# Residual buffers ahead of the sums' buffers, and pinned, paired divisions in the last projection of a four-layer graph kernel

## The chip, the cores and the metric

The kernel runs on one core of one Trainium2 chip. The metric is the device time of one execution in microseconds (us); the time before is the median of three runs. The core has TensorE (PE, with its weight loads shown apart as PEld), VectorE (DVE), ScalarE (ACT), GpSimd (POOL) and SyncE (SP); SP, POOL and ACT also issue DMAs.

## The reference

Four layers run over a graph of 3327 nodes with 512 features and a dense 0/1 adjacency `adj`. Each layer is added to its input and normalized over the features:

```python
x = _layernorm(x + _L0_gnn_ref(x, adj, W, a))             # attention, 8 heads x 64
x = _layernorm(x + _L1_gnn_ref(x, adj, W_nb, ...))        # mean of the first 64 neighbours
x = _layernorm(x + _L2_gnn_ref(x, adj, W, a))             # attention, 8 heads x 64, elu
x = _layernorm(x + _L3_gnn_ref(x, adj, W, a))             # attention, 4 heads x 128, elu

# attention, per head
h = x @ W
e = leaky_relu(h @ a1 [:, None] + h @ a2 [None, :], 0.2)
att = softmax(where(adj > 0, e, NEG))
out = att @ h                                             # then elu in L2 and L3
```

So behind each attention a kernel has, per row, the weighted sums and the sum of the weights: it divides, applies elu where there is one, adds the residual and normalizes.

## The kernel before, in words

**Tiles.** The 3327 rows make 26 tiles (NT) of 128 rows by 512 features. A layer's work between two attentions goes over these tiles; the attention itself goes over pairs of source and destination rows and fills most of the time (L405 on DVE, L408 on ACT, L428 and L380 on PE).

**Where sums are kept.** An attention stores its weighted sums, not yet divided, in `hd` in HBM. The reciprocals of the weights' sums lie in `rec` on chip. For the last half of the last heads these come late: partial sums go through `dd` and sixteen small DMAs (`place`, L517) into `pes`, and `finish_sums` (L523 to L538) makes `rec` of them. `Layer.late` holds these two steps, and the next stage calls them when it is at tiles 4 and 8.

**Finishing a group** (`finish_steps`, from L165). For n tiles from t0 it gives a list of steps:
- `load`: for each tile a buffer `h` filled from `hd` and a buffer `xr` filled with the residual, both through L126; xr always on POOL's queue, h on the queue that the caller names.
- `divide(s)`: h times rec on DVE (L181), and with elu an exponential into `e` on ACT (L186).
- `add(s)`: with elu two DVE operations, min(e,1)+xr into xr (L194) and max(h,0)+xr into h (L195); without, one addition (L197).
- `norm_rows` (L147 to L161): per tile bn_stats (L152) and bn_aggr (L153) on DVE; one square root on ACT for the group (L154); reciprocal (L155) and product (L158) on DVE; and per tile an ACT operation (L161) that scales and shifts h in place.

Exponential and square root belong to different function tables of ACT, so a table load stands where it changes from one to the other.

**The last projection** (`third`, from L892) finishes layer 2's sums and makes what layer 3's attention reads. It has 13 turns of two tiles (t0 = 0, 2, ...). In a turn it
1. calls L2.late at t0 = 4 and 8;
2. loads the group t0+6 (`load_group`);
3. for each of the two tiles: stores it as x3 (L133); `project1` (L253 to L263): four PE transposes (L261) into `pt`, an ACT copy to `xT` (L262), and on DVE the column sums `xsum` (L263); after the first tile only, all steps that finish the group t0+2; then `project2` (L266 to L283) of the tile before: 16 matmuls (L271) into two banks `pw`, on ACT an exponential `dc` (L272) and two copies `rc`, `qc` (L275), on DVE two products `vt` (L277), and the store of v (L283);
4. at tile 14 prepares the first half of the attention (`prepare` L304 to L322, `cut` L324 to L351, `rows` L359).
After the loop come `mean` (L286 to L293) and the attention of layer 3.

The pool `p_f` holds the groups: ten buffers for h, six for xr, two for e.

**What sets the order.** PE's instructions run in the order of the program: `tc.manual_schedule` names PE alone. On the other engines a planner orders them by estimated times when the kernel is built, and they run in that order. `tc.keep_in_program_order(ins)` pins one instruction: on its engine, what is written before it stays before and what is written after it stays after. In `finish_steps` the flag `pinned` pins the exponential of a group's first tile; `third` sets it for the group of tiles 2 and 3 only. A buffer's address is given when its tile is allocated, in the order of the program; a transfer into it waits for whatever last used these addresses.

**The same helper elsewhere.** The second layer's first step (`step1`, `step2`, from L721) finishes layer 0's sums with `finish_steps`, two tiles at a time, without elu and unpinned; layer 3's own end (`later`, from L957) uses it for the first half of the rows. In the first of these, PE transposes a finished tile (L724) and multiplies it with two matrices (L732, L735).

Of the kernel before, what the change touches and what calls it, by code (L numbers as in the profile page):

```python
# [7 lines left out]
F32 = mybir.dt.float32  # L8
# [5 lines left out]
ALU = mybir.AluOpType  # L14
# [4 lines left out]
P = 128  # L19
# [13 lines left out]
def kernel(  # L33
# [10 lines left out]
    nc = tc.nc  # L44
    N, F = x.shape
# [59 lines left out]
    for e in range(2):  # L105
        nc.vector.tensor_tensor(c1w[:, :, e, :], c1[:, :, 8 * e:8 * e + 4], c1[:, :, 8 * e + 4:8 * e + 8],
                                op=ALU.add)
# [4 lines left out]
    rec = const.tile([P, NT, 8], F32, name="rec")  # L112
# [6 lines left out]
    def load_tile(dst, src, t, eng):  # L119

        if src.shape[0] == N and t == NT - 1 and LAST < P:
            nc.gpsimd.memset(dst, 0.0)
            for a, z in _row_pieces(LAST):
                eng.dma_start(out=dst[a:z, :], in_=src[t * P + a:t * P + z, :])
        else:
            eng.dma_start(out=dst, in_=src[t * P:(t + 1) * P, :])  # L126

    def store_tile(dst, src, t, eng):
        if dst.shape[0] == N and t == NT - 1 and LAST < P:
            for a, z in _row_pieces(LAST):  # L130
                eng.dma_start(out=dst[t * P + a:t * P + z, :], in_=src[a:z, :])
        else:
            eng.dma_start(out=dst[t * P:(t + 1) * P, :], in_=src)  # L133
# [7 lines left out]
    def load_wide(t, src, eng):  # L141
        for e in range(2):
            eng.dma_start(out=t[:, :, e, :FW], in_=src[:, e * FW:(e + 1) * FW].rearrange("(c p) m -> p c m", p=P))


    def norm_rows(pool, ys, t0):
        n = len(ys)  # L147
        st = pool.tile([P, 4, 6], F32, name="st")
        mv = pool.tile([P, 4, 2], F32, name="mv")
        rs = pool.tile([P, 4, 2], F32, name="rs")  # L150
        for s, y in enumerate(ys):
            nc.vector.bn_stats(out=st[:, s, :], in_=y)  # L152
            nc.vector.bn_aggr(out=mv[:, s, :], in_=st[:, s, :])  # L153
        nc.scalar.activation(rs[:, :n, 0], mv[:, :n, 1], AF.Sqrt, bias=eps)  # L154
        nc.vector.reciprocal(rs[:, :n, 0], rs[:, :n, 0])  # L155
        if t0 + n == NT:
            nc.vector.tensor_tensor(rs[:, n - 1, 0:1], rs[:, n - 1, 0:1], valid, op=ALU.mult)
        nc.vector.scalar_tensor_tensor(rs[:, :n, 1], mv[:, :n, 0], -1.0, rs[:, :n, 0],  # L158
                                       op0=ALU.mult, op1=ALU.mult)
        for s, y in enumerate(ys):  # L160
            nc.scalar.activation(y, y, AF.Identity, bias=rs[:, s, 1:2], scale=rs[:, s, 0:1])  # L161
# [3 lines left out]
    def finish_steps(pool, xin, layer, t0, n, hbufs=6, eng=nc.sync, xbufs=None, xpool=None, ebufs=None, pinned=False):  # L165
        H, D = layer.H, layer.D
        ys, xs, steps = [], [], []

        def load():
            for t in range(t0, t0 + n):  # L170
                h = pool.tile([P, F], F32, name="h", bufs=hbufs)
                load_tile(h, hd, t, eng)
                ys.append(h)
                xr = xpool.tile([P, F], F32, name="xr", tag="hb") if xpool else \
                    pool.tile([P, F], F32, name="xr", bufs=xbufs)
                load_tile(xr, xin, t, nc.gpsimd)
                xs.append(xr)

        def divide(s):
            h = ys[s]  # L180
            nc.vector.tensor_tensor(h.rearrange("p (h d) -> p h d", h=H), h.rearrange("p (h d) -> p h d", h=H),  # L181
                                    rec[:, t0 + s, :H].rearrange("p (h e) -> p h e", e=1).to_broadcast([P, H, D]),
                                    op=ALU.mult)
            if layer.elu:
                e = pool.tile([P, F], F32, name="e", bufs=ebufs)
                ins = nc.scalar.activation(e, h, AF.Exp)  # L186
                if pinned and s == 0:
                    tc.keep_in_program_order(ins)
                xs.append(e)

        def add(s):
            h, xr = ys[s], xs[s]
            if layer.elu:
                nc.vector.scalar_tensor_tensor(xr, xs[n + s], 1.0, xr, op0=ALU.min, op1=ALU.add)  # L194
                nc.vector.scalar_tensor_tensor(h, h, 0.0, xr, op0=ALU.max, op1=ALU.add)  # L195
            else:
                nc.vector.tensor_tensor(h, h, xr, op=ALU.add)  # L197

        steps.append(load)
        for s in range(n):  # L200
            steps += [lambda s=s: divide(s), lambda s=s: add(s)]
        steps.append(lambda: norm_rows(pool, ys, t0))
        return ys, steps

    def finish(*a):
        ys, steps = finish_steps(*a)
        for f in steps:
            f()
        return ys
# [682 lines left out]
    def third(first):  # L892
        with tc.tile_pool(name="col3", bufs=1) as cp, tc.tile_pool(name="at_r3", bufs=2, reuse_waits="tile") as rp:
# [3 lines left out]
            with tc.tile_pool(name="p_w", bufs=1, reuse_waits="tile") as wp, \  # L897
                    tc.tile_pool(name="p", bufs=3, reuse_waits="tile") as pp, \
                    tc.tile_pool(name="p_f", bufs=2, reuse_waits="tile") as fp, \
                    tc.tile_pool(name="p_ps", bufs=2, space=PSUM, reuse_waits="tile") as ps:  # L900
                wsb = wp.tile([P, FC, 2, FW + L3.H], F32, name="wsb")

                def bank(e):
                    return ps.tile([P, 512], F32, name=f"pw{e}")


                pend = None
                ahead = first
                groups = []

                def load_group(t0):
                    if t0 < NT:
                        groups.append(finish_steps(fp, x2, L2, t0, 2, 10, nc.gpsimd if t0 < 4 else nc.sync, 6,
                                                    pinned=t0 == 2))
                        groups[-1][1].pop(0)()

                load_group(2)
                load_wide(wsb, w3, nc.gpsimd)
                nc.vector.tensor_copy(wsb[:, :, :, FW:], wa[3].rearrange("p c (e h) -> p c e h", e=2))
                load_group(4)  # L920
                for t0 in range(0, NT, 2):
                    ys = ahead
                    if t0 in (4, 8):
                        L2.late.pop(0)(fp)
                    load_group(t0 + 6)
                    for s, y in enumerate(ys):
                        t = t0 + s
                        store_tile(x3, y, t, nc.sync)
                        xT = L3.project1(pp, ps, y, t)
                        if s == 0 and groups:  # L930
                            ahead, steps = groups.pop(0)
                            for f in steps:
                                f()
                        if pend:
                            L3.project2(pp, bank, wsb, *pend)
                        pend = (xT, t)
                        if t == HALF + 1:
                            L3.prepare(pp, 0)
                            L3.first_rows = L3.rows(rp, 0, 0)
                            L3.cut(pp, 0)  # L940
                L3.project2(pp, bank, wsb, *pend)
                L3.mean(pp, bank, wsb)
# [282 lines left out]
```

## Time and profile before

| | |
|---|---|
| median of 3 runs | 3392.79 us (3391.16 to 3394.97) |
| the profiled execution | 3389.15 us, span 3387.4 us |
| mean granted clock of PE | 0.985 |
| busy, share of the span | PE 96%, PEld 48%, DVE 79%, ACT 70%, POOL 7% |
| L405 on DVE | 1040 times, mean 1954 ns |
| L428 on PE | 8320 matmuls, mean 521 ns |
| L271 on PE, all projections | 1248 matmuls, mean 397 ns |
| L154 table loads | 45, mean 1283 ns |

Times in the timeline count from the start of the span. The last projection starts at about 2551 us (its first transposes, L261, at 2555.88) and its last matmul (L293) ends at about 2688 us: some 4% of the span. The layer that finishes L0's sums starts at about 958 us.

In a line of the timeline the first number is the start, the second the duration, then engine, line, operation, what is written and read, shapes, how many of them follow one another, and in brackets the idle time ahead of it and what ended it. In a line of groups the first figure after the count is busy time, the next the mean of one, and after the bar come idle time and its releasers.

### The profile page before, as it was taken

Reading aid. Unit: us, or ns where it says so; the run is one execution under the profiler, and the core shown is the slowest. Engines: PE = TensorE matmul, PEld = TensorE weight load, DVE = VectorE, ACT = ScalarE, POOL = GpSimd, SP = SyncE. Lnnn points to the kernel's source line nnn. Section 1 sums busy time; section 2 is a strip of 40 time slices with the busy share of each in tenths; the row PEclk is TensorE's granted clock in tenths of the full one; section 3 lists DMA queues with packets and bytes.
Section 4 is the critical chain, followed back from the end, with each engine's and each line's share of the span. In section 5 each row is a group of like instructions: output and inputs, shape, how many; then the busy total and the mean of one; then the engine's idle time right before and its main releaser. Section 6 shows DMA issues by size and latency. Waiting matters only on the chain.

```text
span 3387.4 us, 47182 instructions
## 1 busy us (share of the span) xinstructions
PE 3251.2 (96%) x18476; PEld 1626.4 (48%) x18476; DVE 2687.5 (79%) x2619; ACT 2354.6 (70%) x2143; POOL 239.8 (7%) x389
## 2 busy tenths in 40 slices
PE   8899999999979999999989999999998999999997
PEld 7634344444434445545544444444446754455453
DVE  5799999999967544444449999999998766668887
ACT  2398998999953333333338999999997655558986
POOL 3100000000010011111110000000002000010110
PEclk9999999999999999999999999999998999999998
DMA  9644111110143343333320111111117411122211
GB/s 368 222 124 127 49 49 38 55 49 28 44 123 125 122 117 84 91 85 87 80 77 20 47 48 50 51 48 47 35 31 241 152 41 42 41 51 80 94 42 49
DMA packets 288014, 284.29 MB, mean 84 GB/s; under 512 B 107492, under 2 KB 223534, under 8 KB 287791
## 3 DMA queue, kind: packets, MB, share of 16 engines
q1 hardware_dynamic: 254063, 170.62, 16.6%
q0 software_dynamic: 28208, 102.96, 9.5%
q10 hardware_dynamic: 5520, 7.69, 0.7%
q8 instruction: 146, 2.39, 0.3%
q14 instruction: 77, 0.63, 0.1%
HBM read 212.01 MB, written 69.17 MB: 83 GB/s over the span
## 4 chain that ended last, share of the span: by engine, by line
PE 85%; DVE 5%; DMA 4%; ACT 3%; issue 2%; SPq 0%; ACTq 0%; DVEq 0%; POOL 0%; POOLq 0%
PE po L428 52%; PE acc L859 12%; PE pd L380 7%; PE pw L271 5%; DVE t L405 3%; PE pz L732 3%; DMA raw<-in_adjT_dram 3%; PE pi L735 3%; ACT y L408 1%; PE pt L456 1%; PE pk L819 1%; DMA h<-hd 0%; PE pa L1108 0%; PE pt L724 0%; PE pct L664 0%
## 5 line engine op out<-in xcount | busy, mean ns | idle before, releaser
L405 DVE SCALAR_TENSOR_TENSOR t<-rb,qc,mask 128x1664 f32<-128x1664 f32 x1040 | 1960.3, 1954 | 169.4 <-PE po L428 147.3
L408 ACT ACTIVATE y<-t,bi,sc 128x1664 fp8e4<-128x1664 f32 x1040 | 1769.5, 1766 | 310.4 <-PE pd L380 292.7
L428 PE MATMUL po<-t,vj 128*64 128x448 f32 (+3 forms) x8320 | 1909.6, 521 | 22.1 <-DVE t L405 19.6
L428 PEld LDWEIGHTS po<-t,vj 128*64 128x64 f32 (+1 forms) x8320 | 838.9, 148 | 970.6 <-issue 704.0
L859 PE MATMUL acc<-zs,kt 128*128 128x512 bf16 x1352 | 401.1, 380 | 0.0
L271 PE MATMUL pw<-wsb,xT 128*128 128x264 f32 (+1 forms) x1248 | 302.2, 397 | 15.2 <-DVE vt L277 12.0
L859 PEld LDWEIGHTS <-kt 128*128 128x128 fp8e4 x2002 | 196.1, 98 | 242.1 <-issue 7.7
L811 ACT CAST pk<-cy 128x512 f32<-128x512 bf16 x169 | 99.0, 588 | 277.4 <-DVE kt L823 266.3
L271 PEld LDWEIGHTS pw<-wsb,xT 128*128 128x128 f32 x1248 | 241.1, 197 | 60.7 <-ACT xT L262 10.8
L380 PE MATMUL pd<-y,sden 128*32 128x448 fp8e4 (+1 forms) x4160 | 259.5, 342 | 10.4 <-ACT y L408 10.4
L859 PE MATMUL acc<-zl,kt 128*128 128x512 bf16 x650 | 246.5, 379 | 0.0
L380 PEld LDWEIGHTS <-sden 128*32 128x32 bf16 x4160 | 117.5, 96 | 162.5 <-issue 139.8
L823 DVE SCALAR_TENSOR_TENSOR kt<-pk,mask 128x512 fp8e4<-128x512 f32 x169 | 116.1, 688 | 94.0 <-PE pk L819 94.0
L277 DVE TENSOR_TENSOR vt<-pw,dc 128x256 f32<-128x256 f32 x156 | 59.0, 418 | 148.2 <-ACT dc L272 143.7
L359 POOL DMA_DIRECT2D rb<-r x40 | 21.3, 532 | 1670.4 <-DVE t L405 1652.2
L275 ACT COPY rc<-pw 128x8 f32<-128x8 f32 (+1 forms) x78 | 12.6, 162 | 156.6 <-PE pw L271 154.1
L831 DVE SCALAR_TENSOR_TENSOR y<-acc,cnt,bnb 128x512 f32<-128x512 f32 x26 | 19.5, 751 | 97.7 <-PE acc L859 90.3
L732 PE MATMUL pz<-wn,xT 128*128 128x512 f32 x208 | 94.9, 600 | 1.7 <-ACT xT L726 1.7
L700 POOL DMA_DIRECT2D cy<-ctd x91 | 67.9, 746 | 385.1 <-ACT pk L811 312.6
L735 PE MATMUL pi<-wl,xT 128*128 128x512 f32 x208 | 93.5, 592 | 0.0
L634 DVE TENSOR_SCALAR mask<-raw 128x832 fp8e4<-128x832 int32 (+2 forms) x90 | 54.8, 614 | 38.9 <-DMA raw<-in_adjT_dram 38.5
L154 ACT ACT_TABLE_LOAD x45 | 57.7, 1283 | 37.0 <-DVE mv L153 36.4
(187 smaller groups left out, 1699.3 us busy)
## 6 DMA issues: line engine op xcount, KB each, us to landing
vj<-v SPq DMA_DIRECT2D x312, 128.0 KB
rb<-r POOLq DMA_DIRECT2D x40, 832.0 KB, 4.8
raw<-in_adjT_dram SPq DMA_DIRECT2D x67, 416.0 KB
cy<-ctd POOLq DMA_DIRECT2D x78, 256.0 KB, 4.0
h<-hd SPq DMA_DIRECT2D x61, 256.0 KB
v<-vt SPq DMA_DIRECT2D x50, 256.0 KB
hd<-hb SPq DMA_DIRECT2D x48, 256.0 KB
xr<-x POOLq DMA_DIRECT2D x45, 256.0 KB, 3.1
```

Of the source, the lines that this page charges most:

```text
L271: nc.tensor.matmul(pw[e][:, :FW + H], xT[:, c, :], wsb[:, c, e, :], start=c == 0, stop=c == FC - 1)
L277: nc.vector.tensor_tensor(vt[:, hs, :], pw[e][:, :FW].rearrange("p (h d) -> p h d", d=D), self.dc[:, t, hs].rearrange("p (h e) -> p h e", e=1)
L380: nc.tensor.matmul(pd[c][32 * kk:32 * kk + 32, :w_], lhsT, rhs, start=(kk, c) not in seen, skip_group_check=final is not None, stop=last a ...
L405: nc.vector.scalar_tensor_tensor(t, rb[k], self.qc[:, j, h:h + 1], mask[:, j, i0:i0 + IW], op0=ALU.max, op1=ALU.mult)
L408: nc.scalar.activation(y, t, AF.Sigmoid, bias=self.bi[:, j, h:h + 1], scale=self.sc[:, j, h:h + 1], saturate=False)
L428: nc.tensor.matmul(po[c][k * D:(k + 1) * D, :z - a_], vj[:, j % 2, k * D:(k + 1) * D], ts[k][:, a_:z], start=j == 0, stop=j == NT - 1)
L700: nc.gpsimd.dma_start(out=cy[:, :n, :], in_=ctd[t:t + n, b * GW:(b + 1) * GW] .rearrange("(o t) i -> o t i", o=1).to_broadcast([P, n, GW]))
L732: nc.tensor.matmul(pz, xT[:, c, :], wn[:, c, :], start=c == 0, stop=c == FC - 1)
L735: nc.tensor.matmul(pi, xT[:, c, :], wl[:, c, :], start=c == 0, stop=c == FC - 1)
L811: nc.scalar.copy(pks[k % 2], carry[b, t // 4 * 4][:, t % 4:t % 4 + 2, :])
L823: nc.vector.scalar_tensor_tensor(kt, pk, NEIGHBOURS, mask[:, t:t + 2, i0:i0 + GW], op0=ALU.is_le, op1=ALU.mult, saturate=False)
L859: nc.tensor.matmul(acc, kts[t][:, s * P:(s + 1) * P], zs(t, c) if c < 2 else zl[:, t, :], start=t == 0 and c == 0, stop=t == NT - 1 and c ...
```

## The change

In `load` the residual's buffer `xr` is allocated before `h`; the DMAs are issued in the same order as before. With `pinned`, the steps of a group run as divide, divide, add, add instead of divide, add, divide, add, and the division on DVE is pinned for every group but the first (t0 > 2); the exponential is pinned for tile 2 alone, as before. `third` passes `pinned=True` for all its groups. Lines below `add` stand five further down than before (L194 and L195 two, L186 two).

```diff
@@ -168,23 +168,25 @@
 
         def load():
             for t in range(t0, t0 + n):
+                xr = xpool.tile([P, F], F32, name="xr", tag="hb") if xpool else \
+                    pool.tile([P, F], F32, name="xr", bufs=xbufs)
                 h = pool.tile([P, F], F32, name="h", bufs=hbufs)
                 load_tile(h, hd, t, eng)
                 ys.append(h)
-                xr = xpool.tile([P, F], F32, name="xr", tag="hb") if xpool else \
-                    pool.tile([P, F], F32, name="xr", bufs=xbufs)
                 load_tile(xr, xin, t, nc.gpsimd)
                 xs.append(xr)
 
         def divide(s):
             h = ys[s]
-            nc.vector.tensor_tensor(h.rearrange("p (h d) -> p h d", h=H), h.rearrange("p (h d) -> p h d", h=H),
-                                    rec[:, t0 + s, :H].rearrange("p (h e) -> p h e", e=1).to_broadcast([P, H, D]),
-                                    op=ALU.mult)
+            ins = nc.vector.tensor_tensor(h.rearrange("p (h d) -> p h d", h=H), h.rearrange("p (h d) -> p h d", h=H),
+                                          rec[:, t0 + s, :H].rearrange("p (h e) -> p h e", e=1).to_broadcast([P, H, D]),
+                                          op=ALU.mult)
+            if pinned and t0 > 2:
+                tc.keep_in_program_order(ins)
             if layer.elu:
                 e = pool.tile([P, F], F32, name="e", bufs=ebufs)
                 ins = nc.scalar.activation(e, h, AF.Exp)
-                if pinned and s == 0:
+                if pinned and (t0, s) == (2, 0):
                     tc.keep_in_program_order(ins)
                 xs.append(e)
 
@@ -197,8 +199,11 @@
                 nc.vector.tensor_tensor(h, h, xr, op=ALU.add)
 
         steps.append(load)
-        for s in range(n):
-            steps += [lambda s=s: divide(s), lambda s=s: add(s)]
+        if pinned:
+            steps += [lambda s=s: divide(s) for s in range(n)] + [lambda s=s: add(s) for s in range(n)]
+        else:
+            for s in range(n):
+                steps += [lambda s=s: divide(s), lambda s=s: add(s)]
         steps.append(lambda: norm_rows(pool, ys, t0))
         return ys, steps
 
@@ -911,7 +916,7 @@
                 def load_group(t0):
                     if t0 < NT:
                         groups.append(finish_steps(fp, x2, L2, t0, 2, 10, nc.gpsimd if t0 < 4 else nc.sync, 6,
-                                                    pinned=t0 == 2))
+                                                    pinned=True))
                         groups[-1][1].pop(0)()
 
                 load_group(2)
```

In the built programs the instructions of PE have the same order. On DVE, ACT, POOL and SP the order differs within `third` alone; ACT has two more table loads, the other engines the same number of instructions.

## The prediction

> **What bounds the kernel now.** First the page's header and its chain of work that ended last: TensorE (PE) carries the kernel, and the line the change is about shows only in the 5% and 4% that VectorE (DVE) and DMA hold.
>
> ```profile
> span 3387.4 us, 47182 instructions
> PE 85%; DVE 5%; DMA 4%; ACT 3%; issue 2%; SPq 0%; ACTq 0%; DVEq 0%; POOL 0%; POOLq 0%
> ```
>
> A mean over the span says nothing of the last projection, so next the table of busy time in 20 us windows over it (columns: window, length, PE, PEld, DVE, ACT, POOL busy with instruction counts, granted PE clock, DMA share, GB/s).
>
> ```profile
> 2560.00:2580.00 20.00, 11.54 (x37) 9.09 (x36) 15.96 (x36) 13.13 (x23) 2.88 (x6) 0.64 0.88 274
> 2580.00:2600.00 20.00, 20.00 (x102) 17.25 (x101) 18.50 (x44) 16.51 (x34) 3.22 (x6) 1.00 0.82 270
> 2640.00:2660.00 20.00, 20.00 (x103) 17.41 (x102) 17.86 (x48) 17.15 (x40) 1.06 (x2) 1.00 0.67 228
> 2660.00:2680.00 20.00, 20.00 (x103) 17.37 (x103) 8.85 (x17) 8.68 (x25) 0.00 (x0) 1.00 0.25 96
> ```
>
> Only the first window leaves PE idle. After 2580, PE is full, and in the last window DVE has fallen to 8.85 of 20: it finished the normalization of the last tiles before PE needed them. The steady stage is PE's, because DVE and ScalarE (ACT) run ahead. The timeline of PE shows the stage's rhythm and its one large hole.
>
> ```profile
> 2559.27 5.79 PE L271 MATMUL pw<-wsb,xT 128*128 128x260 f32 x14 [0.30 <-DMA wsb<-in_w_dram]
> 2573.51 1.12 PE L261 MATMUL pt<-ident,h 128*128 128x128 f32 x4 [8.46 <-ACT h L161]
> ...
> 2664.64 0.60 PE L261 MATMUL pt<-ident,h 128*128 128x128 f32 x4
> 2665.08 3.67 PE L271 MATMUL pw<-wsb,xT 128*128 128x260 f32 x16
> 2668.59 0.60 PE L261 MATMUL pt<-ident,h 128*128 128x128 f32 x4
> 2669.03 3.67 PE L271 MATMUL pw<-wsb,xT 128*128 128x260 f32 x16
> 2672.54 0.60 PE L261 MATMUL pt<-ident,h 128*128 128x128 f32 x4
> ```
>
> A tile costs PE 3.95 us (0.44 of transposes, 3.51 of projection), two tiles 7.9. Tile 2 starts 8.46 us late, at 2573.51. Who made it late, says the timeline of DVE:
>
> ```profile
> 2557.77 0.68 DVE L263 TENSOR_REDUCE xsum<-xT 128x4 f32<-128x512 f32 x1
> 2562.96 1.40 DVE L181 TENSOR_TENSOR h<-h,rec 128x512 f32<-128x512 f32 x2 [4.52 <-DMA h<-hd]
> 2564.28 0.69 DVE L194 SCALAR_TENSOR_TENSOR xr<-e,xr 128x512 f32<-128x512 f32 x1
> ```
>
> The two divisions at 2562.96 belong to tiles 4 and 5. The planner put them ahead of tile 2's add at 2564.28, and they wait 4.52 us for a load, though tile 2's own exponential (L186) was done at 2559.62.
>
> **What the Trainium skill says.** "Perfetto Trace Analysis", section "Tensor Engine Instruction (MATMUL, LD_WEIGHTS)", calls ACT, DVE and GpSimd strict FIFOs; the last fence is that, tile 2's ready add behind tile 4's late division. "ScalarE: Activation LUTs", "What ACT_TABLE_LOAD costs": about 1.28 us for a load and about 1.38 of drain at each switch of function set. The trace has the 1283 ns, but no such drain: the load at 2570.74 is followed by its exponential at 2572.04. So I charge 1.28. "TensorE: Matmul & The Clock Gate", "What's actually happening": after an idle window of about 3.4 us PE falls to half clock. Here the 8.46 us hole and the 3.64 us hole at 2634.75 are followed by half-clock work (projections of 5.42 and 5.36 instead of 3.67 us); holes of 0.98 and 1.30 us are not.
>
> **The parts.** Line numbers are those of before.
>
> *Residual's buffer ahead of the sum's.* No instruction is added or moved in time by the program; addresses change, and with them what a load waits for. It bears where the first layer's sums are finished. There the load of tile 2's residual on POOL is issued at 969.73 after 9.92 us of idle time; by the built order it waits for the store of a buffer it lies over. Laid elsewhere it can go at about 960. But DVE's order has a division there that lands at 977.21 after 2.25 us for a load which SP issues only at 972.89, behind six other DMAs, and an add of tile 3 stands behind it. PE's hole of 13.84 us before 983.97 hangs on that. So the earlier residual is hidden; what remains is less traffic beside the late load. I take −1 us; bounds −2 and +1.3 (more traffic before, one landing later).
>
> *The start of the last projection.* Divisions are pinned, so tiles 4 and 5 come after tile 2's and 3's adds. Worked: tile 3's exponential ends at 2560.62; its first add then 2560.65; three more DVE slots of 0.60 for the rest of the adds, two for the statistics, to 2563.65, aggregates to 2563.8. Now ACT's order has the three small copies of tile 0's projection first, and PE ends that at 2565.06: 2565.35 after copies, table load to 2566.65, square root 0.30, reciprocal and product 0.31 with hops to 2567.4, normalization (L161) 0.81: PE starts tile 2 at 2568.3 instead of 2573.51, −5.2 us. Late next is PE's own projection of tile 0, which already fills that time.
>
> *The steady stage.* This is where the pin costs. In program order the division of the next group stands after the column sums (L263) of the current group's first tile. Pinned, it can't pass them, so what let DVE run ahead is gone: PE transposes tile t, the sums of t release the divisions of t+2, and their result is what PE transposes next. One turn per two tiles, with durations from the rows of 2575 to 2635: transposes 0.60, copy (L262) 0.59, sums 0.60, division 0.69, exponential 0.63, four adds and two statistics at a slot of 0.60 = 3.60, aggregate, one L277 at its slot, aggregate 0.17+0.34+0.17, square root 0.30, table load 1.28, dc 0.06, normalization 0.81: 9.84, and six hops of some 0.04 between engines: 10.1 us, against PE's 7.9. The table load for the square root is hidden: ACT has time for it during the adds. A second division or exponential lies beside the first add.
> By ACT's built order this form holds for the groups of tiles 4, 6, 8, 20, 22, 24. For 10, 12, 18 the square root stands behind the three copies of the current tile's projection, so PE must first end both tiles: 7.9+0.16 tail, copies 0.27, table load 1.28, square root 0.30, reciprocal and product 0.31, normalization 0.81, hops: 11.2. For 14, two more exponentials (L316, L307, 0.27 and 0.25) and a table load stand in front: 12.5. For 16, with the rows of L312 between, I keep the 14.84 us of before (2626.13 to 2640.97), since its 3.64 us hole covers the new wait.
> Sum from tile 2 to tile 24: 6×10.1 + 3×11.2 + 12.5 + 14.8 = 121.5, against 2672.54 − 2573.51 = 99.0: +22.5. The tail behind tile 24 and the attention after it keep their lengths. Holes of 2.2 us should not cool PE; those of 3.3 (three) and 4.6 (one) may, at some 1.7 us each (a projection at 5.4 instead of 3.7). I take one, +2; bounds 0 and +7.
>
> *Traffic.* DMAs of the stage are the same in number (x3 stores, h, xr, v) and stretched over a longer stage, with POOL's residual loads waiting on the adds as now (55.5 us of POOL's waits); SP's loads of h are asked for two groups before they are divided. Nothing; at worst a load that is late again, up to the 4.5 us seen.
> *Two at a time, and two more ACT instructions* (table loads): inside the turn above.
>
> **Sum.** −1 −5.2 +22.5 +2 = +18.3 us on a profiled execution of 3389.15 (span 3387.4), giving 3407.5. The median of the three runs shown is 3392.79, 3.6 above it; the same addition gives 3411.1.
> Ends of this case: low if group 16 takes 12.5, no hop costs, no cooling, sums of −2: about +10; high with four cooled projections, no gain in the first layer, 0.2 more per turn: about +27. So 3403 to 3420.
>
> **Rivals.** (1) *Pinning removes the blockage and nothing else* (faster). Mechanism: the turn from transposes to normalization stays under 7.9 us, so PE keeps its rhythm. Then −5.2 −1 = 3386.6, at best 3383 with the 3.64 us hole gone too. For it: DVE has 11 of 20 us free at the end and its total work is unchanged. Against: that freedom came from running ahead; the turn is a latency, with ten dependent steps. It decides at 7.9 us for the turn, 2.2 below my sum.
> (2) *The turn is shorter, only dc binds*: normalization stands on ACT behind dc of the current tile, which needs PE to end it: 7.9 + 0.16 + 0.06 + 0.81 + hops = 9.05 in the six groups. Total 115.2, +16.2, net about +10 to +12: 3404. Same sign; it is the low end.
> (3) *Balance*: some groups still slip past, two or three turns of holes (+6) cancel the start (−5): 3394. Against it: the built order has the same pattern in every group.
> (4) *The first layer gains the whole 9.9 us*: if the late load there followed the residual's. 3402; the order on SP speaks against it. That the change does not do what it says can be left out: the built order shows the moved divisions.
>
> **Chances.** A measurement here can tell about 0.2% (6.8 us) from no change. My case with (2) and (4): 0.79; (3) and other small outcomes 0.09; (1) 0.12. Nearly all of the first is slower by more than 0.2%: slower 0.78, same 0.10, faster 0.12. The likeliest case's own range, 3403 to 3420, holds about 0.70; to leave out no more than 2 in 10 it must reach down over (3) to about 3385, into (1).
>
> **What would show it.** Right: in the changed kernel PE's tile 2 starts about 5 us sooner after tile 1, then a hole of 2 to 4 us before every second group of transposes, put down to ACT h L161, and DVE idle waiting for ACT's xT inside the stage; DVE no longer drops to 8.85 at the end. The last projection's end moves from 2688 by about +18. Wrong: holes under 1 us in the steady stage (then (1)); a PE clock of 0.6 to 0.8 through the whole stage (then above 3420); or a first-layer hole of much less than 13.84.

## The result and the profile after

The changed kernel takes 3413.1 us (median of 4 runs, 3409.88 to 3415.64) against 3392.23 for the kernel before on the same chips (4 runs): ratio 1.0066, 95% interval 1.0054 to 1.0078, so 18 to 26 us slower. The profiled execution has a span of 3408.2 us, 20.8 more than before's 3387.4. Lines from L188 on stand a few further down now: L266 are the transposes, L276 the projection, L268 the column sums, L196 and L197 the adds.

The page's header and chain for the changed kernel:

```profile
span 3408.2 us, 47193 instructions
PE 84%; DMA 5%; DVE 5%; issue 3%; ACT 3%; POOL 0%; SPq 0%; ACTq 0%; POOLq 0%; DVEq 0%
```

Shares over the span hardly move. The windows over the last projection do (same columns as before):

```profile
2580.00:2600.00 20.00, 16.98 (x78) 14.20 (x78) 15.71 (x36) 13.62 (x31) 2.15 (x4) 0.91 0.75 235
2660.00:2680.00 20.00, 15.63 (x71) 13.04 (x72) 14.06 (x32) 14.63 (x28) 0.10 (x1) 0.91 0.38 144
2680.00:2700.00 20.00, 15.89 (x80) 13.29 (x79) 13.36 (x35) 12.65 (x28) 0.00 (x0) 1.00 0.28 105
```

Before, PE was busy for 20.00 of 20 from 2640 to 2680 and DVE fell to 8.85. Now no engine is full: PE has 16 to 17, DVE 13 to 16, ACT 13 to 15. A loop that is bound by latency can look like this: every engine waits for another. The timeline of PE tells where:

```profile
2560.49 5.39 PE L276 MATMUL pw<-wsb,xT 128*128 128x260 f32 x14 [0.56 <-DMA wsb<-in_w_dram]
2569.05 1.12 PE L266 MATMUL pt<-ident,h 128*128 128x128 f32 x4 [3.17 <-ACT h L161]
...
2581.02 0.66 PE L266 MATMUL pt<-ident,h 128*128 128x128 f32 x4 [0.96 <-ACT h L161]
...
2591.18 0.66 PE L266 MATMUL pt<-ident,h 128*128 128x128 f32 x4 [2.05 <-ACT h L161]
2591.68 5.36 PE L276 MATMUL pw<-wsb,xT 128*128 128x260 f32 x16
...
2613.22 1.12 PE L266 MATMUL pt<-ident,h 128*128 128x128 f32 x4 [3.17 <-ACT h L161]
2614.13 6.25 PE L276 MATMUL pw<-wsb,xT 128*128 128x260 f32 x16
...
2640.07 1.12 PE L266 MATMUL pt<-ident,h 128*128 128x128 f32 x4 [4.47 <-ACT h L161]
...
2684.34 0.66 PE L266 MATMUL pt<-ident,h 128*128 128x128 f32 x4 [2.06 <-ACT h L161]
```

The first hole, 8.46 us before, is 3.17: tile 2 starts at 2569.05. Then every second tile, that of group 16 apart, waits for its normalization. In the waits of this stage, first one line of the kernel before, then two of the changed kernel:

```profile
PE pt L261 <- ACT h L161: 11.8, 2, 8.5
```

```profile
PE pt L266 <- ACT h L161: 30.4, 12, 4.5
...
DVE xsum L268 <- ACT xT L267: 10.2, 5, 2.7
```

PE waited 11.8 us in two places before, and 30.4 us in twelve now. The last line is the other half of the loop: DVE stands idle for the transposed tile whose sums release its next divisions. The kernel before shows no such wait of DVE in this stage. Both halves in one turn, DVE first, then ACT:

```profile
2582.42 0.68 DVE L268 TENSOR_REDUCE xsum<-xT 128x4 f32<-128x512 f32 x1
2583.01 1.28 DVE L181 TENSOR_TENSOR h<-h,rec 128x512 f32<-128x512 f32 x2
2584.44 1.29 DVE L196 SCALAR_TENSOR_TENSOR xr<-e,xr 128x512 f32<-128x512 f32 x2
2585.65 1.29 DVE L197 SCALAR_TENSOR_TENSOR h<-h,xr 128x512 f32<-128x512 f32 x2
2586.86 1.28 DVE L152 BATCH_NORM_STATS2 st<-h 128x6 f32<-128x512 f32 x2
```

```profile
2588.65 0.29 ACT L154 ACTIVATE rs<-mv,eps 128x2 f32<-128x2 f32 x1 [1.11 <-DVE mv L153]
2588.96 1.28 ACT L277 ACT_TABLE_LOAD   x1
2590.26 0.17 ACT L277 ACTIVATE dc<-pw 128x4 f32<-128x4 f32 x1
2590.32 1.51 ACT L161 ACTIVATE h<-h,rs 128x512 f32<-128x512 f32 x2
```

From the transposes at 2581.02 through sums, two divisions, four adds, two statistics, square root, table load, dc and normalization to the transposes at 2591.18: 10.16 us.

### The profile page after: what moved, and what is told of

Read it like the earlier page. It is cut to its first block, busy times and chain, and to the rows that moved or that the text cites. A ratio compares the mean times of both kernels' runs of the same rounds, so it can differ in the third digit from the quotient of the medians.

```text
span 3408.2 us, 47193 instructions
## 1 busy us (share of the span) xinstructions
PE 3260.6 (96%) x18476; PEld 1630.8 (48%) x18476; DVE 2687.5 (79%) x2619; ACT 2360.1 (69%) x2145; POOL 239.3 (7%) x389
## 4 chain that ended last, share of the span: by engine, by line
PE 84%; DMA 5%; DVE 5%; issue 3%; ACT 3%; POOL 0%; SPq 0%; ACTq 0%; POOLq 0%; DVEq 0%
PE po L433 52%; PE acc L864 12%; PE pd L385 7%; PE pw L276 5%; DVE t L410 3%; DMA raw<-in_adjT_dram 3%; PE pz L737 2%; PE pi L740 2%; ACT y L413 1%; PE pk L824 1%; PE pt L461 1%; DMA r<-rr 0%; PE pa L1113 0%; PE pt L266 0%; DMA v<-vt 0%
## 5 line engine op out<-in xcount | busy, mean ns | idle before, releaser
L276 PE MATMUL pw<-wsb,xT 128*128 128x264 f32 (+1 forms) x1248 | 308.6, 403 | 13.0 <-DVE vt L282 11.1
L276 PEld LDWEIGHTS pw<-wsb,xT 128*128 128x128 f32 x1248 | 245.7, 200 | 60.7 <-ACT xT L267 9.9
```

The lines of the kernel that those rows point to most:

```text
L276: nc.tensor.matmul(pw[e][:, :FW + H], xT[:, c, :], wsb[:, c, e, :], start=c == 0, stop=c == FC - 1)
```

## The experiments

Each ran on one chip together with runs of the kernel before; differences below are the ratio of the runs, with its 95% interval, times the median of before there (3391.36, 3391.04 or 3389.22 us).

**e1, the layout alone.** In the kernel before, `load` allocates xr ahead of h, as the change does. The built order of every engine is that of before.

> The kernel before with one edit: the residual's buffer is allocated ahead of the sum's. No instruction changes its place in the built order, so only waits of loads change. Main theory: it is worth next to nothing; within 2 us of before (the prediction took -1, with -2 to +1.3 as bounds; the changed kernel's trace, where the hole of PE before the second group of the first layer's finishing is 14.98 us instead of 13.84, points to 0 to +2). Rival, that a part of the 20.9 us comes from the layout: +5 or more. Rival, that the early residual is worth its 9.9 us of waiting and the pins cost 30: -8 or less. In the trace the last projection should be as in before, tile 2 at about 22 us after the stage's first transposes.

Measured: +3.7 us (+1.4 to +6.1), a small cost. The middle value lies between the main theory's 2 us and the rival's 5, and the interval reaches both. The traces put 2.2 us of it in the first layer's finishing (34.92 us from its first transposes to tile 3's instead of 32.70) and 0.2 in the last projection. SP's queue and PE of the kernel before:

```profile
961.81 0.33 SPq L507 DMA_DIRECT2D dd<-red  x1
...
968.92 3.87 SPq L517 DMA_DIRECT2D pes<-dd  x6
```

```profile
983.97 1.11 PE L724 MATMUL pt<-ident,h 128*128 128x128 f32 x4 [13.84 <-ACT h L161]
984.87 4.83 PE L732 MATMUL pz<-wn,xT 128*128 128x512 f32 x8
```

and with the layout alone:

```profile
963.43 0.33 SPq L507 DMA_DIRECT2D dd<-red  x1
...
973.13 3.85 SPq L517 DMA_DIRECT2D pes<-dd  x6
```

```profile
986.85 1.11 PE L724 MATMUL pt<-ident,h 128*128 128x128 f32 x4 [15.09 <-ACT h L161]
987.75 5.79 PE L732 MATMUL pz<-wn,xT 128*128 128x512 f32 x8
```

The loads of tiles 2 and 3 no longer wait on POOL (issued at 960.89 to 962.49). They travel beside the small store dd, and the reading back of dd, for which SP waits, starts 9.70 us after the store instead of 7.11. That the traffic is what delays it is the likely reading, but no run takes the traffic away and keeps the layout. Tile 4's load stands behind that, and DVE's next division behind tile 4's load. PE's hole grows from 13.84 to 15.09, and what follows it runs longer at half clock. The four kernels with the layout and without another edit there have 14.98 to 15.09 (the changed kernel, e1, e4, e6), the three without it 13.84 to 13.94 (before, e2, e5).

**e2, pins and pairs without the layout.** The changed kernel with h allocated ahead of xr again.

> The changed kernel with the layout undone: pins and pairs alone, built order of all engines as in the changed kernel. Main theory: the whole effect is here, +18 to +23 us against before, with the same holes ahead of the transposes of tiles 4, 6, 8, ..., 24 as in the changed kernel (1 to 4.5 us each). Rival, that layout and pins act together: more than 4 us away from the changed kernel's +20.9.

Measured: +21.7 us (+17.6 to +25.8), the holes as in the changed kernel. Pins and pairs together carry the effect; no run has the pairs alone. With e1's +3.7 the sum would be 25.4 where the changed kernel has 22.4; the intervals are too wide to tell whether the two add.

**e4, one group ahead.**

```diff
-                ahead = first
+                done = [first]
...
-                    ys = ahead
+                    ys = done.pop(0)
...
-                        if s == 0 and groups:
-                            ahead, steps = groups.pop(0)
+                        while s == 0 and groups and len(done) < 2:
+                            ready, steps = groups.pop(0)
                             for f in steps:
                                 f()
+                            done.append(ready)
```

> The changed kernel, but a group is finished one turn sooner: in the turn of tiles t0 and t0+1 the steps of group t0+4 run instead of those of t0+2. Pins, pairs and layout stay. Main theory: the cost of the pin is the latency of the turn from transposes to the next normalization (10.1 us against PE's 7.9); spread over two turns it need not be shorter than 15.8, so most of the holes close: 14 to 20 us less than the changed kernel, +1 to +6 against before. What is left are normalizations queued on ACT behind the small copies of the current tile. Rival, that the pinned order costs DVE or ACT throughput (more table loads, colder PE) whatever the distance: within 5 us of the changed kernel.

Measured: +8.8 us (+5.4 to +12.2), 13 to 14 less than the changed kernel. Its timeline of PE:

```profile
2593.89 0.66 PE L266 MATMUL pt<-ident,h 128*128 128x128 f32 x4 [1.48 <-ACT h L161]
2597.89 0.60 PE L266 MATMUL pt<-ident,h 128*128 128x128 f32 x4
2603.47 0.65 PE L266 MATMUL pt<-ident,h 128*128 128x128 f32 x4 [1.48 <-ACT h L161]
```

These two turns are 9.59 and 9.58 us long. The later ones lie between 8.4 and 9.8, the one with the preparation apart (14.90), and from tile 2 to tile 24 it takes 110.1 us (2571.89 to 2681.96) instead of 125.5. The same pins at a distance of two turns cost far less: it is the distance that counts, and throughput falls as a reason. Two misses: the gain is at or just under the low end of what was expected, and the time against before is above it, in part perhaps because the layout's 3.7 us had not been reckoned in. In the first turns the holes that are left end with a normalization that stands on ACT behind the current tile's copies, two table loads and an exponential of a later group. After tile 10's transposes PE waits instead ahead of its projections, mostly for xT and rc on ACT and for vt and mv on DVE.

**e5, hold back only at the start.** The kernel before (its layout, no pins on divisions), with all later divisions of the last projection queued on DVE behind the product L158 of tiles 2 and 3 (`tc.issue_after`). e7 to e11 use the same tie.

```diff
+            with tc.issue_after(gate[0]) if gate and layer.li == 2 else nullcontext():
-            nc.vector.tensor_tensor(h.rearrange(...
+                nc.vector.tensor_tensor(h.rearrange(...
...
+        def norm():
+            last = norm_rows(pool, ys, t0)
+            if pinned:
+                gate.append(last.ins)
```

> The kernel before (no layout, no pairs, no pins on divisions), with all later divisions of the last projection queued on DVE behind the product (L158) of the first group, tiles 2 and 3, and otherwise free. Main theory: the start keeps its gain of about 5 us and DVE may run ahead again after it, so 2 to 5 us less than before, 3387 to 3390; tile 2 starts near 2568.5, and holes afterwards are few. Rival, that the start's gain is taken back by a later wait (the copies of rows in the preparation at tile 14, or a turn that is late): within 1.5 us of before. Rival, that holding back the divisions at the start already costs the later turns: +5 or more.

Measured: +1.4 us (−1.4 to +3.7). The rival holds. Counted from the stage's first transposes, tile 2 comes after 12.53 us (17.63 before), and at tile 14 it is still 3.7 us ahead (66.59 against 70.25). It loses that between tiles 14 and 16:

```profile
2626.22 3.75 PE L280 MATMUL pw<-wsb,xT 128*128 128x260 f32 x16 [1.21 <-DVE vt L286]
2631.74 1.04 PE L321 MATMUL pr<-ident,rc 128*4 128x128 f32 x8 [1.77 <-ACT rc L316]
2636.75 1.23 PE L321 MATMUL pr<-ident,rc 128*4 128x128 f32 x5 [3.98 <-ACT rr L323]
2637.77 1.06 PE L270 MATMUL pt<-ident,h 128*128 128x128 f32 x4
```

It takes 19.07 us from tile 14 to 16 instead of 14.84: the preparation waits for rc and then for rr, which stands on ACT behind another group's square root and normalization. The work after these holes ran in part at half clock.

**e6, no square root.** The changed kernel, with ACT's Identity in place of Sqrt in the last projection's groups: the square root is left out, and with it the change of function table. ACT's order changes too, as the planner orders it anew.

> The changed kernel, in which the square root of the last projection's groups (ACT, L154) is left out: the variance with eps is passed on as it is, so no function table is changed in that stage. Main theory: the turn loses its table loads and keeps the queue on ACT. By the built order the normalization now stands behind the three small copies of the current tile's projection in every group, so a turn is 7.9 of PE + 0.16 tail + copies 0.27 + reciprocal and product 0.31 + normalization 0.81 + hops = about 9.5 us for all groups, instead of 10.1, 11.2 and 12.5, with holes of about 1.6 us: 10 to 17 us less than the changed kernel, and still 4 to 12 above before. Rival, that the latency through DVE is all: the turn falls to some 8.5 us and the time to within 3 us of before. Rival, that table loads are hidden: within 4 us of the changed kernel.

Measured: +5.8 us (+3.1 to +8.5) against before, 14 (by the medians) to 17 (by the ratios) less than the changed kernel.

```profile
2603.27 0.66 PE L266 MATMUL pt<-ident,h 128*128 128x128 f32 x4 [1.54 <-ACT h L161]
2607.27 0.60 PE L266 MATMUL pt<-ident,h 128*128 128x128 f32 x4
2612.92 0.66 PE L266 MATMUL pt<-ident,h 128*128 128x128 f32 x4 [1.54 <-ACT h L161]
```

Seven turns are 9.65 or 9.66 us long where 9.5 was worked out, and after these holes of 1.5 us the projections run at full clock. The number came, but not for the reason given: the copies of the current tile are done at 2602.00, and the normalization waits on for DVE.

```profile
2602.40 1.52 ACT L161 ACTIVATE h<-h,rs 128x512 f32<-128x512 f32 x2 [0.41 <-DVE rs L158]
```

```profile
2601.63 0.67 DVE L268 TENSOR_REDUCE xsum<-xT 128x4 f32<-128x512 f32 x1
2602.22 0.15 DVE L158 SCALAR_TENSOR_TENSOR rs<-mv,rs 128x2 f32<-128x2 f32 x1
```

So the table load is a term of the turn, but the changed kernel's turns of 10.16 and 10.18 us to groups 6 and 22 lose only 0.5 of its 1.28: the load had covered the reciprocal, a column sum and the product on DVE, and without it these end the wait. The turns of 11.3 us lose 1.6 to 1.7, and the half-clock work of the changed kernel's turns that end in groups 8, 12 and 20 is not there.

**e7 to e11, the same fault in the first layer.** The holes of 13.84 to 15 us of e1 hang on a division of tile 4 that stands on DVE ahead of tile 3's addition. e7 is the kernel before with e5's tie in layer 0's finishing instead (divisions of tiles 4 and later behind L158 of tiles 2 and 3); e8 adds the layout; e9 adds e5's tie too. The division and the addition in the kernel before:

```profile
977.21 0.69 DVE L181 TENSOR_TENSOR h<-h,rec 128x512 f32<-128x512 f32 x1 [2.25 <-DMA h<-hd]
977.82 0.68 DVE L197 TENSOR_TENSOR h<-h,xr 128x512 f32<-128x512 f32 x1
```

> The kernel before, its layout too, with one tie in the finishing of layer 0's sums: the divisions of tiles 4 and later stay on DVE behind the product (L158) of tiles 2 and 3. Nothing else. Theory: what makes PE's hole of 13.84 us there is the division of tile 4, which stands on DVE ahead of tile 3's addition and waits for a late load. Without that, tile 3's addition goes when its residual has landed, about 974.8 in the time of the kernel before; statistics, square root, normalization to about 978; tile 2 reaches PE at 978 instead of 983.97: hole about 8, 5 to 7 us less than before. Rival, that the residual's own landing and not the division ends the wait: within 2 us of before.

> As the run before it (tie in the first layer's finishing), with the residual's buffer laid ahead of the sum's. Theory: with the tie, the early residual is no longer hidden. Tile 3's division was at 970.99 in the layout's own run, its addition can follow at once, PE gets tile 2 some 4 us after it ran dry instead of 15: hole 3 to 6 us, 8 to 11 us less than before; a layout that alone cost 4 us then gains 3 to 5. Rival, that the added traffic of the early loads costs whatever the order is: no better than the run without the layout, by 1 to 4 us worse.

> As the run before it, and the same tie in the last projection (divisions of tiles 4 and later behind the product of tiles 2 and 3, no pins after it). Theory: the last projection's tie alone gave nothing (+1.4 us, -1.4 to +3.7: tile 2 started 5.1 us sooner and the preparation's holes took it back), so this is within 3 us of the run before it, 6 to 11 us less than before, faster than both kernels. Rival, that the two gains add: 11 us or more.

Measured: e7 −1.4 us (−4.1 to +1.4), e8 −2.0 (−4.7 to +0.7), e9 −1.7 (−4.4 to +1.0), each less than expected and none clear by itself. The holes did shrink: 13.84 before, 11.09 in e7, 9.16 in e8, 8.80 in e9, so the layout that cost when alone is worth 1.9 us of hole with the tie. Who ends the wait now? In e7 it is in part the rival, the residual's own landing: tile 2's addition waits for it.

```profile
975.64 0.69 DVE L201 TENSOR_TENSOR h<-h,xr 128x512 f32<-128x512 f32 x1 [5.01 <-DMA xr<-in_x_dram]
```

In e8, where the residual is early, it is on ACT:

```profile
974.01 0.30 ACT L770 CAST cf<-cr 26x128 f32<-26x128 bf16 x1 [9.13 <-DMA cr<-ctd]
974.23 0.59 ACT L745 CAST zs<-pz 128x512 bf16<-128x512 f32 x1
```

A small cast, needed only at tile 8, waits for its load, and tile 0's zs behind it; DVE's r and tile 3's addition wait for zs. e10 is e8 with this cast kept in its written place, e11 the same with e5's tie.

```diff
-                        nc.scalar.copy(cf, cr)
+                        tc.keep_in_program_order(nc.scalar.copy(cf, cr))
```

> As the kernel with the first layer's tie and the layout, plus one more tie: the cast of the neighbour counts (cf from cr) on ACT is kept in its written place, at tile 8, where it stood ahead of tile 0's cast zs in the built order and waited 9.13 us for its load, to 974.01, with DVE's r (L747 there) and tile 3's addition queued behind. Theory, the same as for the divisions: a queued instruction that waits for a late load holds ready work behind it. Without it the zs cast can go when PE ends pz (about 968.5), tile 3's addition about 971.6, tile 2 reaches PE at about 976.5 instead of 980.74: hole about 5 instead of 9.16, another 3 to 5 us, so 5 to 10 us less than before. Rival, that zs waits for other loads of its own buffer anyway: within 1.5 us of the run without this tie, hole still about 9.

> The same with the last projection's tie too (divisions of tiles 4 and later behind the product of tiles 2 and 3). Theory: last projection again worth 0 to -2 us net, since the preparation's holes at tile 14 take back what tile 2 wins; 5 to 11 us less than before. Rival, that it costs as in its run alone: 1 to 3 us worse than the run before it.

Measured: e10 −6.1 us (ratio 0.9982, 0.9974 to 0.9991), e11 −5.1 us (0.9985, 0.9978 to 0.9992). Both are faster than before, by less than 0.2% but clear of noise, and faster than the changed kernel. PE in e10:

```profile
976.01 1.11 PE L733 MATMUL pt<-ident,h 128*128 128x128 f32 x4 [5.97 <-ACT h L161]
```

The hole is 5.97 us, near the 5 that was expected. From the first layer's first transposes to those of tile 4 it is 31.91 us (960.65 to 992.56) instead of 40.01 before. Within the hole, the normalization now waits 2.00 us for DVE's product (L158), which stands behind four operations for tile 0 (L750 to L755). Whether the last projection's tie helps beside it can't be told from these runs.

## Why the prediction was right, point by point

**Size.** Forecast +18.3, from medians +20.9. Term by term in the two profiled executions:

| term | forecast | measured |
|---|---|---|
| first layer | −1 | +1.6 (34.34 instead of 32.70 from its first transposes to tile 3's) |
| start, to tile 2 | −5.2 | −4.7 (12.96 instead of 17.63) |
| tile 2 to tile 24 | +22.5, and +2 for cooling | +26.4 (125.45 instead of 99.03) |
| tile 24 to the mean's matmuls | 0 | +0.1 (11.90, 11.84) |

From its first transposes to the mean's matmuls the last projection takes 21.8 us more, where the forecast's terms for it make 19.3. The sum, +23.4, is 2.6 more than the spans differ by: in this execution the first attention ended 2.6 us sooner than in before's, 955.66 against 958.28 (starts 955.12 and 957.74, both 0.54 long), ahead of all that was changed. The runs do not say why; single executions of the kernel before differ by as much (3391.16 to 3394.97).

**The turn.** This was the step that decided, and it held. Turns that end in groups 4, 6, 8, ..., 24:

```
group     4     6     8    10    12    14    16    18    20    22    24
forecast 10.1  10.1  10.1  11.2  11.2  12.5  14.8  11.2  10.1  10.1  10.1
measured 11.97 10.16 10.76 11.28 14.27 12.58 11.33 11.34 11.42 10.18 10.16
```

Six agree within 0.15 us. e4 shows that it is the distance of one turn that makes the latency count, e6 that the table load is a term of it. e2, with the same pins, has 10.16 us for group 8, 11.28 for 10 and 11.34 for 18.

**Mis-sized terms.** (1) Group 16 was kept at before's 14.84 us because its hole would cover the new wait. It took 11.33: the rows' transposes, which waited 3.64 us before, now wait 0.23, since rr on ACT came in time. (2) Cooling was taken as one stretch, 2 us, and the forecast said holes of 2.2 us should not cool PE. They can: a projection partly at half clock (5.36 us) follows the hole of 2.05 at 2591.18, and transposes of 1.12 us that of 3.17 at 2613.22, while 3.17 at 2627.49 and the holes of 2.06 and 2.05 at 2684.34 and 2694.50 are followed by 3.67. Turns 4, 8, 12 and 20 exceed the forecast by 6.9 together; each has half-clock work in it, so by estimate cooling is worth about 7, the forecast's outer bound. e2 bears this out: its turn to group 12 has no half-clock projection and takes 11.58 us instead of 14.27, while its turn to group 14 has one and takes 14.26 instead of 12.58. The two errors, −3.5 and +5, nearly cancel, so that the total came so near is in part luck; that the turns did is not. (3) The first layer: −1 was taken, +1.3 was the bound given for more traffic ahead of a late landing. The sign was wrong: there was more traffic ahead of the late load and not less beside it, and what happened is near that bound (hole +1.14 here, +1.25 in e1). The matmuls behind the hole are longer too, 5.76 us instead of 4.83.

**Rivals.** The faster one was to be decided at 7.9 us for the turn; no turn was below 10. The one in which only dc binds (9.05) did not hold either. e4 and e6, where turns fall to 9.6, show what comes next: the queue on ACT in e4, the product on DVE in e6. No group slipped past, as the third rival had it. The whole 9.9 us of the first layer did not come, for the reason given; e10 shows that 8 us of that stretch are to be had once the residual is early and what stands in the way on both DVE and ACT is moved.

**Two corrections.** The prediction says that PE is full after 2580. It is not: it names the hole of 3.64 us at 2634.75 itself, and there are those of 0.98 and 1.30. Its 99.0 us from tile 2 to 24 was read from the trace and holds them. The text ahead of the prediction says that a pin keeps everything written before ahead and everything written after behind. The changed kernel's trace shows that it binds less. L541 and L543 are written at the head of the turn of tiles 8 and 9 (`finish_sums`), ahead of the pinned divisions of tiles 10 and 11, and run behind them:

```profile
2604.31 0.68 DVE L181 TENSOR_TENSOR h<-h,rec 128x512 f32<-128x512 f32 x1
2604.91 0.20 DVE L541 SCALAR_TENSOR_TENSOR rec<-pes,rec 128x52 f32<-128x52 f32 x1
2605.03 0.68 DVE L181 TENSOR_TENSOR h<-h,rec 128x512 f32<-128x512 f32 x1
2605.63 0.79 DVE L543 RECIPROCAL rec<-rec 128x104 f32<-128x104 f32 x1
```

The order fits a pin that ties an instruction only to the one written just ahead of it on its engine. For the pinned division that is the column sums, so the turn is the same. e5 needs all later divisions held back, and uses another tie.

## What to carry to other kernels

A pin that stops a queued wait in one place holds in every turn of a loop: add up the latency of one turn from release to release and set it against the bounding engine's time per turn, for here the turn of 10.16 us against PE's 7.9 cost the difference nearly every time. Work that runs ahead hides such latencies; a sign of it is an engine that ends early, as DVE did before. If a ready instruction stands behind one that waits for a load, move that one instruction, and then look who waits next: here the kernel with three blockers moved, on DVE, in a load's buffer and on ACT, was the first whose time moved clearly (e10). Whether it needs all three is not shown, as the third was not moved without the other two.

## What the runs showed of the hardware

Half-clock stretches did not need a hole of 3.4 us, which the prediction cited from the Trainium skill, "TensorE: Matmul & The Clock Gate", section "What's actually happening": a hole of 2.05 us in the changed kernel was followed by 5.36 us for a projection instead of 3.67. So in these traces a shorter hole than the page's can be enough, and the measurement decides. Nor does the length alone tell: holes of 2.05, 2.06 and 3.17 us in the same stage (at 2694.50, 2684.34 and 2627.49) were followed by 3.67. In e6 the regular holes of 1.54 us cooled nothing, and the last one, of 1.94, was followed by 5.36. What decides between 1.9 and 3.2 us no run here shows.

The small store dd of 112 KB and the first reading back of it started 7.11 to 7.19 us apart in the four kernels (before, e2, e5, e7) where POOL still held back four loads of 256 KB, and 9.50 to 9.74 in the eight where these were issued ahead of the store or beside it.
